# A graph layer's segment maximum: fewer nodes by chunk scans, more by slots, and an iota of 96 columns between gathers

## The chip, the core and the metric

One core of one Trainium2 chip runs the whole kernel. TensorE (PE in the profile, PEld for its weight loads), VectorE (DVE), ScalarE (ACT), GpSimd (POOL) and SyncE (SP) run side by side and wait for one another through semaphores. The metric is the device time of one execution in microseconds (us); before the change it is 1135.02 us, the median of three runs (1132.8 to 1135.32).

## The reference

```
x_src = x[src];  x_dst = x[dst]                       # 100000 edges, sorted by dst
theta_x = (x_dst - x_src) @ theta_w.T + theta_b
phi_x = x_src @ phi_w.T + phi_b
e = relu(theta_x + phi_x)                             # 100000 x 256
out = segment_max(e, dst, num_segments=6250)
out = where(isfinite(out), out, 0.0)
return layernorm(x + out)
```

`x` has 6250 rows (nodes) of 256 floats. Within one node's segment `x_dst` is the same, so the kernel doesn't compute an edge at a time. It computes `b = x @ (phi_w - theta_w).T + theta_b + phi_b` and `a = x @ theta_w.T` once for each node; a node's result is `max(0, a[node] + max of b[src] over its edges)`, and 0 where it has no edges. What remains is an irregular maximum: for each of 6250 nodes the elementwise maximum over the rows of `b` that its edges (16 on average) name.

## The kernel before

The line numbers are those of the kernel before. Two methods share the nodes out, and some leftovers of the second form a third stream of work.

*By chunk scans (part 1).* The first `N1` = 6250 - 128 x 32 = 2154 nodes. Their edges lie in `dst` order; each of the 128 partitions takes 275 edges in a row (`FIRST_STEPS`, `T1`). In step t every partition gathers the row of `b` that its edge t names (`gather`, L467, an indirect DMA issued by POOL, one descriptor a partition), and DVE takes the running maximum with the row of the step before (`run`, L722); a column of `caps_1` cuts the running maximum off where a new node begins. Eight steps form a group (`STEPS`, `gather_group` L490, `group_1` L728), which fills one of seven tiles of a ring (`RING`), and is written to `maxima_1` in DRAM by SP. Five of the 35 groups (`X_GROUPS`) don't wait for `b_rows`: they gather rows of `x` before it exists and are multiplied by the weights on chip (`b_of`, L663). A segment that crosses from one partition to the next is put right at the end (`chunk_heads`, `tails_1`, `heads_1` L829: one gather from `maxima_1`, one maximum, one scatter back).

*By slots.* The last 4096 nodes, 32 for each partition (`TILES`). A window of `dst` (640 entries a partition, `WINDOW`, gathered by `gather_run`, L475) tells each partition where its nodes begin: `begin` (L623 to L632) counts the entries below each of 33 limits by one ACT operation of sign and sum for each. Then one gather for each of the 32 node columns brings a table of up to 36 source numbers a node (`table_i`, `R` = 36). The rows of `b` are cut into 17 *slots* of 375 rows. For a slot, `choice` (L877) finds for every node the lowest source that lies in it, and `wanted` (L912) writes these choices to DRAM as a row of 4096 numbers. `slot_part` (L939) then fetches the chosen rows, for 1024 nodes at a time, by matmul instead of by DMA: SP broadcasts the 1024 numbers over the partitions (`want`), DVE (L949) and ACT (L951, L952) turn them into one-hot matrices (`hot`), PE multiplies the slot's 375 rows (`terms`, two parts of the float32 value for accuracy) with them (L959, 24 matmuls of 512 columns), and DVE takes the maximum into `acc` (L970), which holds the result transposed. A slot is loaded by `slot_terms` (L926) into `raw` and split by ACT and DVE. 17 slots of 4 pieces of 1024 nodes are 68 parts.

*The list.* Where a node has a second source in the same slot, `choice` leaves it over. `list_pieces` (L980) packs the leftovers of each partition into a list of up to 240 (`LIST`); `group_2` (L1044) gathers and scans these in 30 groups of 8, as in part 1.

*Rows.* `rows_of` (L1051) computes `a` for up to eight tiles of 128 nodes, gathers the nodes' maxima, joins in `acc` and adds `x`; `normalise` (L1096) does the layernorm and writes `out`. `node_place` (L762) and `places_1` find, for part 1's 17 tiles, where in `maxima_1` a node's maximum lies.

The order of issue on each engine is that of the program; a tile framework adds the waits. The preparation (up to about L700) makes the tables on DVE, ACT and POOL while PE makes `b_rows`. Then the schedule (L1120 to L1193) interleaves by hand: the nine `choice` calls with two part-1 groups each and one slot part in the first; `list_pieces` with a slot part for each of its pieces; the rest of the part-1 groups at 1.2 slot parts a group (`PACE`); the list groups at 1.2 slot parts a group, with the tail work of part 1 in between; what is left of the slot parts; and last the rows of the slot nodes (in shares of 8, 8, 8, 4, 2, 1 and 1 tiles).

```
1152    places_1()
1153    carried = tails_1()
1154    lists = list(range(0, LIST, STEPS))
1155    for i in range(2):
1156        group_2(lists.pop(0))
1157        fetch_parts(1)
1158    heads_1(carried)
```

Of the kernel before, what the change touches and what calls it, by code (L numbers as in the profile page):

```python
# [52 lines left out]
RING = 7  # L53
GENERAL_STEPS = 17
FIRST_STEPS = 275
X_GROUPS = 5
X_BEFORE = 2
TILES = 32
LIST = 240
WINDOW = 640  # L60
# [5 lines left out]
PACE = 1.2  # L66
# [339 lines left out]
def gnn_kernel(ctx: ExitStack, tc: tile.TileContext, x, src, dst, theta_w, theta_b, phi_w, phi_b, out):  # L406
# [4 lines left out]
    Q = N // P  # L411
    LEFT = N - P * Q
    NT = Q + 1
    XQ = 4
# [8 lines left out]
    NB = N // ROWS  # L423
    NS = -(-NB // KB)
# [4 lines left out]
    assert D == 2 * P and LEFT > 0 and LEFT1 > 0 and Q % XQ == 0 and OWN % CW == 0  # L429
    assert (P - 1) * T + 1 < E <= P * T and N < ID_MASK and P * T <= EDGES and E + 8 * P <= EDGES  # L430
    assert N == NB * ROWS and SLOT * NS < ABSENT and KB * P <= SLOT and WINDOW <= 8 * P and P * T1 < E
    assert LIST % STEPS == 0 and TILES <= 32
# [12 lines left out]

    x_main = x[: P * Q, :].rearrange("(p q) d -> p q d", q=Q)
    b_main = b_rows[: P * Q, :].rearrange("(p q) d -> p q d", q=Q)
    b_block = b_rows.rearrange("(b r) d -> r b d", r=ROWS)


    x_1 = x[: P * Q1, :].rearrange("(p q) d -> p q d", q=Q1)
    x_2 = x[N1:, :].rearrange("(p q) d -> p q d", q=TILES)
    out_1 = out[: P * Q1, :].rearrange("(p q) d -> p q d", q=Q1)
    out_2 = out[N1:, :].rearrange("(p q) d -> p q d", q=TILES)
    maxima_1t = maxima_1[: P * T1, :].rearrange("(p t) d -> p t d", t=T1)
    maxima_2t = maxima_2[: P * LIST, :].rearrange("(p t) d -> p t d", t=LIST)

    def iota(t, step, base, per_partition):
        nc.gpsimd.iota(
            t,  # L460
            pattern=[[step, t.shape[1]]],
            base=base,
            channel_multiplier=per_partition,
            allow_small_or_imprecise_dtypes=True,
        )

    def gather(to, table, offsets):  # L467
        nc.gpsimd.indirect_dma_start(  # L468
            out=to, out_offset=None, in_=table, in_offset=bass.IndirectOffsetOnAxis(ap=offsets, axis=0)
        )  # L470

    def gather_run(to, table, offsets):

        n = to.shape[1]
        nc.gpsimd.indirect_dma_start(  # L475
            out=to,
            out_offset=None,
            in_=flat(table, 0, [[n, EDGES // n], [1, n]]),
            in_offset=bass.IndirectOffsetOnAxis(ap=offsets, axis=1),
        )  # L480
# [16 lines left out]
    for i in of_x[:X_BEFORE]:  # L497
        gather_group(i, x)
# [28 lines left out]

    weights = const.tile([P, 2, KC, D], FP, name="weights")
    bias = const.tile([P, 1, D], FP, name="bias")

# [13 lines left out]
    with (  # L544
# [4 lines left out]
        with tc.If(n_unsorted > 0):  # L549
            sort_edges(nc, sort, ps_sort, src, dst, src_list, dst_list, ident)  # L550
            load_chunks(nc.sync, dst_i, dst_list, T, EDGES)
            load_chunks(nc.sync, dst_1, dst_list, T1, EDGES)
            load_rows(nc.scalar, src_1, src_list, P * T1)
            for i in of_x[:X_BEFORE]:
                gather_group(i, x)
# [51 lines left out]
    accs = body.enter_context(tc.tile_pool(name="accs", bufs=1))  # L607
    acc = accs.tile([P, KC, OWN], FP, name="acc")
    index = body.enter_context(tc.tile_pool(name="index", bufs=1))
    dst_w = index.tile([P, WINDOW], I32, name="dst_w")  # L610
    gather_run(dst_w, dst_list, edge0_i)
    for i in of_x[X_BEFORE:]:
        gather_group(i, x)
# [9 lines left out]
    BATCH = 8  # L623
    for j0 in range(0, TILES + 1, BATCH):
        j1 = min(j0 + BATCH, TILES + 1)
        for j in range(j0, j1):
            junk = index.tile([P, WINDOW], BF, name="junk")
            nc.scalar.activation(  # L628
                junk, local, AF.Sign, bias=halves[:, j : j + 1], scale=-1.0, accum_out=sums[:, j : j + 1]
            )  # L630
        nc.vector.tensor_scalar(begin[:, j0:j1], sums[:, j0:j1], 0.5, 0.5 * WINDOW, op0=ALU.mult, op1=ALU.add)
# [8 lines left out]

    with (
        tc.tile_pool(name="prep", bufs=1) as prep,
        tc.tile_pool(name="x_in", bufs=3) as x_in,
# [5 lines left out]
        for i, w in enumerate((theta_w, phi_w)):  # L649
            nc.sync.dma_start(w_in[:, i], w.rearrange("(c p) k -> p c k", p=P))  # L650
        biases = prep.tile([P, 2, D], FP, name="biases")
        for i, b in enumerate((theta_b, phi_b)):
            nc.sync.dma_start(biases[:, i, :], flat(b, 0, [[0, P], [1, D]]))
        nc.vector.tensor_add(bias[:, 0, :], biases[:, 0, :], biases[:, 1, :])
        nc.vector.tensor_sub(w_in[:, 1], w_in[:, 1], w_in[:, 0])
        for i in (1, 0):
            for c in range(KC):
# [3 lines left out]
                nc.vector.tensor_copy(weights[:, i, :, c * P : (c + 1) * P], ps[:, 0])  # L661

        def b_of(to, rows):  # L663

            n = rows.shape[1]
            ps = ps_t.tile([P, 2, KC, P], FP, name="ps_xt")
            for i in range(n):
                for k in range(KC):
                    nc.tensor.transpose(ps[:, i, k, :], rows[:, i, k * P : (k + 1) * P], ident)
            x_t = prep.tile([P, 2, KC, P], FP, name="x_t", bufs=3)  # L670
            nc.scalar.copy(x_t[:, :n], ps[:, :n])  # L671
            ps = ps_b.tile([P, 2, D], FP, name="ps_b")
            for i in range(n):
                for k in range(KC):
                    nc.tensor.matmul(  # L675
                        ps[:, i, :], x_t[:, i, k, :], weights[:, 1, k, :], start=(k == 0), stop=(k == KC - 1)
# [3 lines left out]
        for q in range(0, NT, XQ):  # L680
            n = min(XQ, NT - q)
            b_sb = b_out.tile([P, XQ, D], FP, name="b_sb")
            x_q = x_in.tile([P, XQ, D], FP, name="x_q")
            if q < Q:
                nc.sync.dma_start(x_q, x_main[:, q : q + XQ, :])
            else:
                nc.vector.memset(x_q[:, 0, :], 0.0)
                nc.sync.dma_start(x_q[:LEFT, 0, :], x[P * Q :, :])
# [3 lines left out]
            if q < Q:  # L692
                nc.scalar.dma_start(b_main[:, q : q + XQ, :], b_sb)
            else:
                nc.scalar.dma_start(b_rows[P * Q :, :], b_sb[:LEFT, 0, :])
        for i in of_x:
            for k in range(0, STEPS, 2):
                rows = ring_tiles[i][:, k : k + 2, :]
# [15 lines left out]
    ps_fetch = fetch.enter_context(tc.tile_pool(name="ps_fetch", bufs=3, space=PSUM))  # L714
    last = {1: None, 2: None}
# [113 lines left out]
    def heads_1(carried):  # L829
        heads = work.tile([P, D], FP, name="heads", bufs=1)  # L830
        at_heads = bass.IndirectOffsetOnAxis(ap=head_i[:, 0:1], axis=0)
        nc.gpsimd.indirect_dma_start(out=heads, out_offset=None, in_=maxima_1, in_offset=at_heads)
        nc.vector.tensor_tensor(heads, heads, carried, op=ALU.max)
        nc.gpsimd.indirect_dma_start(out=maxima_1, out_offset=at_heads, in_=heads, in_offset=None)
# [10 lines left out]
    BATCH_S = 2  # L845

# [6 lines left out]
    def sources():  # L853
        nc.vector.tensor_copy(source.rearrange(by_rank, r=R), table_i.rearrange("p j r -> p r j"))
        floor_of(work_1, source, ROWS)
        floor_of(work_2, work_1, KB)
        nc.vector.scalar_tensor_tensor(source, work_1, float(P - ROWS), source, op0=ALU.mult, op1=ALU.add)
        nc.vector.scalar_tensor_tensor(source, work_2, float(SLOT - KB * P), source, op0=ALU.mult, op1=ALU.add)
        nc.gpsimd.iota(
            rank.rearrange(by_rank, r=R),  # L860
            pattern=[[1, R], [0, TILES]],
            base=0,
            channel_multiplier=0,
            allow_small_or_imprecise_dtypes=True,
        )
# [6 lines left out]
        nc.vector.scalar_tensor_tensor(work_1, source, float(-ABSENT), work_2, op0=ALU.add, op1=ALU.mult)  # L872
        nc.vector.tensor_scalar(padded, work_1, float(ABSENT), None, op0=ALU.add)
        nc.vector.memset(unused, 1)


    def choice(s0):  # L877
# [17 lines left out]
        at = index.tile([P, BATCH_S, 1, TILES], I16, name="at")  # L895
        for i in range(n):
            blocks = min(KB, NB - (s0 + i) * KB)
            nc.vector.tensor_scalar(
                at[:, i, 0, :], low[:, i, :W], (blocks - 1) * P + ROWS, None, op0=ALU.min
            )  # L900
        nc.vector.tensor_copy(chosen[:, s0 : s0 + n, :], at[:, :n, 0, :])
# [24 lines left out]
    def slot_terms(s):  # L926

        blocks = min(KB, NB - s * KB)
        f = raw
        even = ROWS // 16 * 16  # L930
        nc.sync.dma_start(f[:even, :blocks, :], b_block[:even, s * KB : s * KB + blocks, :])
        nc.sync.dma_start(f[even:ROWS, :blocks, :], b_block[even:, s * KB : s * KB + blocks, :])
        terms = terms_of[s] = slots.tile([P, PARTS, KB, D], FR, name="terms")
        nc.scalar.copy(terms[:, 0, :blocks], f[:, :blocks])
        nc.vector.tensor_tensor(
            terms[:, 1, :blocks], f[:, :blocks], terms[:, 0, :blocks].bitcast(FP), op=ALU.subtract
        )

    def slot_part(s, c):  # L939
        if c == 0:  # L940
            slot_terms(s)
        blocks = min(KB, NB - s * KB)
# [4 lines left out]
        for b in range(blocks):  # L947
# [5 lines left out]
        for h in range(KC):  # L953
            ps = ps_fetch.tile([P, CW], FP, name="ps_f")
            n = blocks * PARTS
# [23 lines left out]

    def list_pieces():  # L980
        left_over = index.tile([P, BATCH_S, TR], I16, name="in_slot")[:, 0, :]
        nc.vector.scalar_tensor_tensor(left_over, padded, float(ABSENT), unused, op0=ALU.is_lt, op1=ALU.mult)
        valid, count, place, name = work_1, work_2, rank, source
# [7 lines left out]
        nc.gpsimd.iota(  # L991
            place, pattern=[[1, TR]], base=1, channel_multiplier=0, allow_small_or_imprecise_dtypes=True
        )
        nc.vector.tensor_tensor(count, place, count, op=ALU.subtract)
        nc.vector.tensor_tensor(count, count, valid, op=ALU.mult)
        distance = place.bitcast(I32)
        nc.vector.tensor_copy(distance, count)
        nc.vector.tensor_scalar(distance, distance, 19, None, op0=ALU.logical_shift_left)
        nc.gpsimd.iota(
            name.rearrange(by_node, r=R),  # L1000
            pattern=[[1 << ID_BITS, TILES], [0, R]],
            base=1,
            channel_multiplier=0,
            allow_small_or_imprecise_dtypes=True,
# [30 lines left out]
        has = work.tile([P, TILES], FP, name="has_2")  # L1035
# [190 lines left out]
```

## Time and profile before

| what | value | from |
|---|---|---|
| runs | 1132.8, 1135.02, 1135.32 us | three timed runs |
| profiled execution | 1127.47 us, span 1125.6 us | one execution, the one that all rows below are from |
| granted TensorE clock | 0.788 | mean over the span |
| slot matmuls, PE, L959 | 1600 of 436 ns, 444.9 us | groups |
| gathers of `b_rows` for part 1, POOL, L468 | 235 of 1184 ns, 278.3 us | groups |
| gathers of `b_rows` for the list, POOL, L468 | 240 of 986 ns, 236.6 us | groups |
| scans, DVE, L722 | 513 of 478 ns, 244.3 us | groups |
| maxima into `acc`, DVE, L970 | 128 of 1215 ns, 155.5 us | groups |
| one-hot matrices, ACT, L951 and L952 | 132 of 1145 and 132 of 1050 ns, 280.0 us | groups |
| one-hot matrices, DVE, L949 | 68 of 748 ns, 50.9 us | groups |
| counts, ACT, L628 | 33 of 830 ns, 27.4 us | groups |
| wait of POOL ahead of L832's gather | 23.4 us, for a write of `maxima` | groups |

The page draws the span in 40 slices of 28.1 us, a digit being the busy tenths of a slice (9 is 90% or more):

```
PE   0466893585147403295829328578185785986273
PEld 0355783364135302173607216456164664764262
DVE  1221693799978621184758118276165584994164
ACT  0256220564114210075655105276254463830175
POOL 6735377488888777554524754667555756204500
```

The stages lie so: preparation up to about 143 us, choice and list with the first groups of part 1 to about 396, the rest of part 1's groups to about 542, the list groups to about 1020, the rows of the slot nodes to the end. How to read the prediction's rows: a group's row gives an instruction's line, engine, operation and tile, how often it ran, its busy sum and mean; a row of waits gives what the engine's instruction waited for, "remote" and "issue" standing for time that the profile can't put down to another instruction's end; a row of a stretch gives its busy time on each engine and the count of instructions in it.

### The profile page before, as it was taken

The numbers are of one execution on the slowest core, as the hardware profiler recorded it, in microseconds if no ns is written. First come the engines' busy times: TensorE is split into PE (matmuls) and PEld (weight loads), VectorE is DVE, ScalarE is ACT, GpSimd is POOL, SyncE is SP. The second block draws the span as 40 slices with busy tenths as digits, with TensorE's granted clock in tenths as the row PEclk, the third lists the DMA queues.
The fourth block names the chain that finished last, engine by engine and source line by source line (L and its number), as shares of the span: only waits on it lengthen the run. The fifth ranks groups of instructions, "written<-read, shape, count | busy, mean of one in ns | idle before, by whom it ended". The sixth has DMA issues, their size and how long they took to land. (4 is left out here: it accounts for less than half of the span.)

```text
span 1125.6 us, 9291 instructions
## 1 busy us (share of the span) xinstructions
PE 651.4 (58%) x2557; PEld 503.6 (45%) x2557; DVE 630.7 (56%) x1309; ACT 429.2 (38%) x680; POOL 640.3 (57%) x622
## 2 busy tenths in 40 slices
PE   0466893585147403295829328578185785986273
PEld 0355783364135302173607216456164664764262
DVE  1221693799978621184758118276165584994164
ACT  0256220564114210075655105276254463830175
POOL 6735377488888777554524754667555756204500
PEclk9888996787668756596959757889586977988696
DMA  6445365477455645264738627566275665735222
GB/s 213 128 138 165 113 193 179 140 254 238 169 173 190 201 144 166 77 221 128 229 122 290 188 81 226 165 220 213 85 238 182 219 202 189 240 144 215 80 99 92
DMA packets 63082, 195.61 MB, mean 174 GB/s; under 512 B 14071, under 2 KB 22795, under 8 KB 53515
## 3 DMA queue, kind: packets, MB, share of 16 engines
q1 hardware_dynamic: 32207, 112.01, 28.3%
q0 software_dynamic: 28272, 75.14, 23.2%
q10 hardware_dynamic: 2540, 7.75, 1.8%
q8 instruction: 23, 0.38, 0.1%
q14 instruction: 40, 0.33, 0.1%
HBM read 114.27 MB, written 81.38 MB: 174 GB/s over the span
## 5 line engine op out<-in xcount | busy, mean ns | idle before, releaser
L959 PE MATMUL ps_f<-hot,terms 128*128 128x512 f32 x1600 | 444.9, 436 | 293.7 <-DVE hot L949 123.0
L959 PEld LDWEIGHTS ps_f<-hot,terms 128*128 128x128 f32 x1600 | 334.6, 213 | 392.5 <-issue 222.9
L468 POOL DMA_INDIRECT g<-b_rows,src x235 | 278.3, 1184 | 118.1 <-issue 67.7
L468 POOL DMA_INDIRECT g<-b_rows,list_src x240 | 236.6, 986 | 148.2 <-issue 72.3
L970 DVE TENSOR_TENSOR acc<-acc,ps_f 128x1024 f32<-128x1024 f32 x128 | 155.5, 1215 | 252.5 <-remote 228.7
L951 ACT ACTIVATE hot<-want,minus_row 128x1024 fp32r<-128x1024 f16 x132 | 146.1, 1145 | 323.3 <-remote 200.3
L722 DVE SCALAR_TENSOR_TENSOR g<-g,caps 128x256 f32<-128x256 f32 x513 | 244.3, 478 | 27.5 <-DMA g<-b_rows,src 9.7
L952 ACT ACTIVATE hot<-hot 128x1024 fp32r<-128x1024 f32 x132 | 133.9, 1050 | 0.4
L675 PE MATMUL ps_b<-weights,x_t 128*128 128x256 f32 x356 | 94.1, 421 | 55.0 <-ACT x_t L671 43.0
L468 POOL DMA_INDIRECT g<-maxima,place x49 | 47.1, 961 | 109.3 <-issue 62.0
L675 PEld LDWEIGHTS ps_b<-weights,x_t 128*128 128x128 f32 x356 | 72.9, 211 | 73.5 <-ACT x_t L671 48.2
L1077 PE MATMUL ps_e<-weights,x_t 128*128 128x256 f32 x128 | 37.4, 440 | 39.2 <-ACT x_t L1073 37.3
L671 ACT COPY x_t<-ps_xt 128x512 f32<-128x512 f32 (+1 forms) x45 | 24.9, 577 | 76.3 <-remote 31.1
L949 DVE TENSOR_SCALAR hot<-want,row_id 128x1024 fp32r<-128x1024 f16 x68 | 50.9, 748 | 1.3 <-ACT hot L952 1.3
L475 POOL DMA_INDIRECT table_i<-src_list,begin_i x32 | 30.2, 944 | 34.0 <-DVE begin_i L632 24.5
L468 POOL DMA_INDIRECT g<-in_x_dram,src x40 | 38.5, 964 | 15.9 <-issue 11.3
L1077 PEld LDWEIGHTS ps_e<-weights,x_t 128*128 128x128 f32 x128 | 25.9, 213 | 47.1 <-ACT x_t L1073 41.2
L678 DVE TENSOR_TENSOR b_sb<-ps_b,bias 128x512 f32<-128x512 f32 (+1 forms) x25 | 16.7, 677 | 52.3 <-PE ps_b L675 22.9
L1104 ACT ACTIVATE squares<-g,r 128x256 bf16<-128x256 f32 x49 | 24.3, 498 | 47.7 <-issue 39.8
L628 ACT ACTIVATE junk<-local,halves 128x640 bf16<-128x640 f32 x33 | 27.4, 830 | 32.1 <-DVE b_sb L678 16.3
L1087 DVE TENSOR_TENSOR g<-g,ps_e 128x512 f32<-128x512 f32 (+1 forms) x17 | 11.1, 655 | 48.7 <-PE ps_e L1086 23.7
L1073 ACT COPY x_t<-ps_e 128x512 f32<-128x512 f32 (+1 forms) x17 | 9.4, 553 | 61.0 <-PE ps_e L1071 38.3
(194 smaller groups left out, 511.1 us busy)
## 6 DMA issues: line engine op xcount, KB each, us to landing
maxima<-g SPq DMA_DIRECT2D x64, 1024.0 KB
want<-chosen_rows SPq DMA_DIRECT2D x68, 256.0 KB
x_q<-in_x_dram SPq DMA_DIRECT2D x12, 512.0 KB
b_rows<-b_sb ACTq DMA_DIRECT2D x12, 512.0 KB
raw<-b_rows SPq DMA_DIRECT2D x16, 336.0 KB
g<-in_x_dram SPq DMA_DIRECT2D x5, 1024.0 KB
out_dram<-g SPq DMA_DIRECT2D x5, 1024.0 KB
g<-b_rows,list_src POOLq DMA_INDIRECT x240
```

Of the source, the lines that this page charges most:

```text
L468: nc.gpsimd.indirect_dma_start(out=to, out_offset=None, in_=table, in_offset=bass.IndirectOffsetOnAxis(ap=offsets, axis=0))
L475: nc.gpsimd.indirect_dma_start(out=to, out_offset=None, in_=flat(table, 0, [[n, EDGES // n], [1, n]]), in_offset=bass.IndirectOffsetOnAxis ...
L628: nc.scalar.activation(junk, local, AF.Sign, bias=halves[:, j : j + 1], scale=-1.0, accum_out=sums[:, j : j + 1])
L671: nc.scalar.copy(x_t[:, :n], ps[:, :n])
L675: nc.tensor.matmul(ps[:, i, :], x_t[:, i, k, :], weights[:, 1, k, :], start=(k == 0), stop=(k == KC - 1))
L722: nc.vector.scalar_tensor_tensor(g[:, k, :], last[part], caps[:, t : t + 1], g[:, k, :], op0=ALU.min, op1=ALU.max)
L949: nc.vector.tensor_scalar(hot[:, b, :], want, row_id[:, b : b + 1], None, op0=ALU.is_equal)
L951: nc.scalar.activation(hot[:, b, :], want, AF.Abs, bias=minus_row[:, b : b + 1], scale=1.0)
L952: nc.scalar.activation(hot[:, b, :], hot[:, b, :].bitcast(FP), AF.Relu, bias=1.0, scale=-1.0)
L959: nc.tensor.matmul(ps[:, w : w + 512], terms[:, part, b, h * P : (h + 1) * P], hot[:, b, w : w + 512], start=(i == 0), stop=(i == n - 1),)
L970: nc.vector.tensor_tensor(to, to, ps, op=ALU.max)
L1077: nc.tensor.matmul(a[:, i, :], x_t[:, 2 * i + c, :], weights[:, 0, c, :], start=(c == 0), stop=(c == KC - 1))
```

## The change

Nodes are shared out otherwise: 40 a partition go by slots (5120 instead of 4096), and 1130 instead of 2154 by chunk scans, of 146 steps instead of 275. With that the window grows from 640 to 800 entries, the list from 240 to 288, a slot has five pieces of 1024 nodes instead of four (85 parts instead of 68), and part 1 has 9 tiles of nodes instead of 17. Three groups of part 1 gather `x` (five before), one of them ahead of the branch that sorts unsorted edges (two before).

POOL's order is written out: `in_turn` ties each gather, and each iota behind it, to the one before by a dependency without a semaphore, and behind every gather stands an iota of 96 columns into a tile that nothing reads:

```diff
+    pause = const.tile([P, PAUSE], FP, name="pause")
+    latest = [None]
+
+    def in_turn(one):
+        if latest[0] is not None:
+            after = mybir.DependencyInfo(mybir.DependencyClass.NoSync, mybir.DependencyReason.DATA)
+            tc.add_manual_dep(one.ins, latest[0], after, reason="GpSimd's order")
+        latest[0] = one.ins.name
+
+    def indirect(out, in_, in_offset=None, out_offset=None):
+        in_turn(nc.gpsimd.indirect_dma_start(out=out, out_offset=out_offset, in_=in_, in_offset=in_offset))
+
     def gather(to, table, offsets):
-        nc.gpsimd.indirect_dma_start(
-            out=to, out_offset=None, in_=table, in_offset=bass.IndirectOffsetOnAxis(ap=offsets, axis=0)
-        )
+        indirect(to, table, bass.IndirectOffsetOnAxis(ap=offsets, axis=0))
+        in_turn(iota(pause, 1, 0, 0))
```

`gather_run` gets the same two lines, and the two iotas of `list_pieces` take their turn in this order. The constants:

```diff
-RING = 7
-FIRST_STEPS = 275
-X_GROUPS = 5
-X_BEFORE = 2
-TILES = 32
-LIST = 240
-WINDOW = 640
+RING = 4
+RING_2 = 7
+FIRST_STEPS = 146
+X_GROUPS = 3
+TILES = 40
+LIST = 288
+WINDOW = 800
...
-PACE = 1.2
+PACE = 2.2
+PAUSE = 96
```

Part 1 has a ring of four tiles; the list and the rows have one of seven (`ring_2`), in the room that the index tables leave when the list is made. Half of the counting moves to DVE, in batches of ten limits instead of eight:

```diff
+    BATCH, BY_SIGNS = 10, 5
...
+            junk = index.tile([P, WINDOW], BF, name="junk" if j < jm else "junk_v")
+            if j < jm:
+                nc.scalar.activation(
+                    junk, local, AF.Sign, bias=halves[:, j : j + 1], scale=-1.0, accum_out=sums[:, j : j + 1]
+                )
+            else:
+                nc.vector.tensor_scalar(
+                    junk, local, halves[:, j : j + 1], None, op0=ALU.is_le, op1=ALU.add, accum_out=begin[:, j : j + 1]
+                )
```

A slot's rows lie otherwise in the partitions: three contiguous rows of `b` in each, instead of three blocks of 125 rows, so that each partition's piece of the load is one run (`slot_terms`); `sources` computes a source's place in its slot accordingly, with one operation more, and its iota of ranks moves ahead into the preparation. Each slot part now has three blocks, the last slot's too.

`b_rows` is made in shares of up to four node tiles of part 1 and of the slot nodes each (`shares`, `node_rows`), instead of 48 tiles over all the nodes and one rest; the columns of `weights` for `b` and `a` change places. The last rows go in five shares of eight tiles.

The schedule:

```diff
     for s0 in range(0, NS, BATCH_S):
         choice(s0)
         wanted(s0)
-        for _ in range(2):
-            group_1(groups_1.pop(0))
-        if s0 == 0:
-            fetch_parts(1)
+        next_group_1(1)
     chunk_heads()
...
     for i, _ in enumerate(list_pieces()):
         if i % 2:
-            group_1(groups_1.pop(0))
-        fetch_parts(1)
-    pace = 0.0
-    while groups_1:
...
+            next_group_1(1)
+    tables.close()
+    ring_2 = body.enter_context(tc.tile_pool(name="ring_2", bufs=RING_2, side="right"))
+    while groups_1 or todo:
+        next_group_1(2)
     places_1()
     carried = tails_1()
...
+    heads = heads_1(carried)
+    for i in range(LIST // STEPS):
+        group_2(i * STEPS)
         pace += PACE
-        while pace >= 1.0:
-            fetch_parts(1)
-            pace -= 1.0
-        if len(lists) % 3 == 0 and (shares or waiting):
+        fetch_parts(int(pace))
+        pace -= int(pace)
+        if i in (3, 5):
+            next(heads, None)
+        if i > 6 and i % 3 == 0 and (early_shares or waiting):
```

`next_group_1(n)` issues a group of part 1, one `node_place` and n slot parts. `heads_1` is a generator now: its gather and its maximum come behind the fourth list group, its scatter behind the sixth (both behind the second before).

## The prediction

> **What bounds the kernel now.** I read the page's busy times first, then the engine-by-stretch table, then the waits, then PE's own timeline. No engine is the bound over the whole span:
>
> ```profile
> PE 651.4 (58%) x2557; PEld 503.6 (45%) x2557; DVE 630.7 (56%) x1309; ACT 429.2 (38%) x680; POOL 640.3 (57%) x622
> ...
> 0.00:143.00 143.00, 76.49 (x349) 62.45 (x350) 43.49 (x98) 44.46 (x95) 75.97 (x97) 0.92 0.48 149
> 143.00:396.00 253.00, 141.45 (x549) 109.62 (x547) 206.89 (x422) 83.20 (x99) 194.21 (x151) 0.77 0.59 194
> 396.00:542.00 146.00, 69.07 (x238) 51.25 (x239) 57.29 (x112) 47.18 (x77) 84.04 (x84) 0.68 0.49 152
> 542.00:1020.00 478.00, 312.91 (x1186) 239.30 (x1185) 280.40 (x519) 212.49 (x293) 255.19 (x259) 0.80 0.58 189
> 1020.00:1125.60 105.60, 51.48 (x242) 40.94 (x240) 42.65 (x161) 41.91 (x119) 30.89 (x32) 0.76 0.35 121
> ```
>
> The columns are length, busy PE, PEld, DVE, ACT, POOL, clock, DMA share, GB/s. Only 143 to 396 has a full engine (DVE, 82%). From 396 to 1020 everything is half idle, so the question is who waits for what:
>
> ```profile
> DVE acc L970 <- remote: 228.7, 21, 24.4
> PEld ps_f L959 <- issue: 222.9, 57, 32.3
> ACT hot L951 <- remote: 200.3, 12, 56.9
> ```
>
> The three columns are microseconds, times, longest. Two stretches (columns as above) and PE's timeline:
>
> ```profile
> 398.00:415.00 17.00, 0.00 (x0) 0.00 (x0) 0.00 (x0) 0.00 (x0) 12.78 (x14) 0.50 0.41 125
> 873.00:890.00 17.00, 17.00 (x77) 14.08 (x76) 13.69 (x23) 10.58 (x12) 13.13 (x13) 1.00 0.86 274
> ...
> 457.31 0.58 PE L959 MATMUL ps_f<-hot,terms 128*128 128x512 f32 x1 [1.50 <-issue]
> 460.11 0.59 PE L959 MATMUL ps_f<-hot,terms 128*128 128x512 f32 x1 [2.21 <-issue]
> 462.21 0.58 PE L959 MATMUL ps_f<-hot,terms 128*128 128x512 f32 x1 [1.51 <-issue]
> ```
>
> DVE and ACT wait over 200 us for something that the profile can't place, and PE's weight loads 223 us for nothing visible. The last lines show it: a matmul every 2.1 to 2.8 us with no wait for any engine. In that stretch POOL issues gathers back to back: 0.95 us each, 0.30 us between, period 1.25. DVE and ACT wait for PE's sums, and wake together at 476.92, 7.7 us after POOL's last gather (468.30 + 0.95). The same comes in the preparation (POOL's run ends at 58.5, PE's sums arrive at 62.4), at 197.3 and 201.3, at 519.4 and 522.9, and in the tail (1060.9, and 1069.5 for the next DVE sum). So uninterrupted gathers hold PE up. They need not: the 873 to 890 line has 13 gathers beside a full PE, at a mean period of 1.31, and from 142.97 to 165.42 sixteen gathers of period 1.40, stretched by DVE's work, run beside a PE busy 24.6 of 26 us; PE stalls when the period falls to 1.25. Which is cause and which effect the trace doesn't say: a stalled PE idles DVE, and then nothing stretches the gathers.
>
> **The change, part by part.**
>
> The pause. Every gather is followed by an iota of 96 columns (L464, held in order by in_turn). POOL's timeline prices it:
>
> ```profile
> 21.25 0.94 POOL L468 DMA_INDIRECT g<-in_x_dram,src  x1 [0.30 <-issue]
> 22.49 0.94 POOL L468 DMA_INDIRECT g<-in_x_dram,src  x1 [0.30 <-issue]
> ...
> 23.99 0.63 POOL L459 IOTA columns<- 128x128 f32 x3
> 24.57 0.23 POOL L459 IOTA ids<- 128x1 f32 x2
> ```
>
> Three iotas of 128 columns take 0.58 us from start to the next start, 0.193 each; small ones follow every 0.10; 96 columns interpolate to 0.165. A POOL operation starts as the gather before it ends (23.44, 58.52). Whether the 0.30 us ahead of the next gather stays is not shown: the period is 0.945 + 0.165 = 1.11 if it hides, 1.41 if it stays. I take 1.41, the nearer to what POOL shows after every gather. That is the period at which PE ran well. The new kernel gathers rows 483 times (146 + 288 + 49), this one 564 (40 + 235 + 240 + 49), so POOL needs 681 us instead of 705 at 1.25: nothing net. At 1.11 it would be 536, and no slower than now, but then the period is the one at which PE stalls.
>
> A rule speaks against it. The Trainium skill, SBUF — State Buffer, section "Who interferes with whom", says that VectorE's two-port modes and GpSimd exclude one another for a whole instruction. The rows agree in kind: gathers average 1.184 us beside the busy DVE of 143 to 542 and 0.986 later, against 0.945 alone. By the rule, were every second iota to sit out one 0.75 us compare (L949), the 299 gathers of the list stage would cost 112 us more, and the sum below would be 1103.
>
> Preparation (A), 143 us now up to the first gather of b_rows. POOL has 8 gathers ahead of the branch instead of 16: 8 x 1.41 = 11.3 against 19.9, with the rank iota of 1440 columns moved there (1.6), so 7 us earlier. The window gather (L475, now L484) stood behind 17 gathers (27.29 to 48.62); now it stands behind 8, at 20.3 + 11.3 = 31.6, and lands 3.5 later, at 35.1, not 52.1. Eight more x gathers end at 44.3, then 40 table gathers x 1.41 = 56.4, to 101. The counts that feed them no longer hold them up: of 10, five on ACT at 1.23 (0.83 x 800/640 + 0.19) and five on DVE, about 8 us against 14 of gathers. b_rows itself: 25 pairs of tiles at 2.31 us (5.45 + 1.47 for three pairs, 84.74 on) = 58 us from about 30, so 88 without stalls, 131 with today's (138 - 7). A = 104, bounds 101 and 131.
>
> Choice, list and first gathers (B), bound by DVE. Tables grow from 1152 to 1440 columns, 1.25 times: sources 16.8 (11.3 now, one more operation), choice 64 (54), list pieces 60 (48). Scans: 145 x 0.478 = 69. Corrections of x groups: 12 x 0.681 = 8. Of 85 slot parts (17 slots x 5), 22 are issued here (16 groups with one, 3 with two): 22 x 0.748 + 17 x 2 x 1.215 + 5 x 0.94 = 62. Node places and the rest 8. Sum 288; from 200 to 375, the stretch of the same work, DVE was busy 159.8 of 175 us, 91%, so 316. Bounds 288 and 346 (the stall of 170 to 200 stays, +30). The fixed order puts list_pieces' two iotas behind 48 gathers of b_rows, at most 48 x 1.65 = 79 us into B; DVE comes to them after choice, later, and waits for neither. POOL's 122 gathers at even 1.65 are 201, hidden; if DVE were free, PE's 22 x 6 = 132 would be next.
>
> List stage (C): 63 parts and 36 groups of gathers. What a part costs is read from two rows:
>
> ```profile
> 825.00:1000.00 175.00, 133.96 (x525) 105.27 (x524) 0.85 0.64 207
> ...
> 975.00:1000.00 25.00, 22.95 (x100) 18.65 (x99) 0.98 0.63 237
> ```
>
> These are the slot matmuls (L959), 24 a part. The second row gives 25 x 24/100 = 6.0 us a part with POOL nearly idle, the first 8.0 with stalls in it; 542 to 1020 gives 478 x 24/1044 = 11.0. Per group of 2.2 parts, PE needs 13.2 at 6.0; POOL 8 x 1.41 = 11.3; DVE 8 x 0.478 + 2.2 x (0.748 + 2 x 1.215 + 0.19) = 11.2; ACT 2.2 x 4.55 = 10.0. Four engines so nearly level don't overlap fully: I take 7.2, so 63 x 7.2 = 454; bounds 378 and 504 without stalls. POOL's 299 x 1.41 = 422 lies beside it. The parts run out after 29 of 36 groups, with POOL up to six groups ahead: 12 us of scans and the last write. The wait of 23.4 us (L832, POOL for the writes of maxima) goes, since that gather now stands behind four groups; DVE waits less for gathers in turn. The larger share of slots is 17 parts more than now (17 x 7.2 = 122), against 81 gathers and scans fewer.
>
> Tail (D): 105.6 now; without its stall (24.7 of DVE's idle time between 1042.6 and 1069.5) 81; four more pairs of tiles at 3.6 (1069.5 to 1104.3 for ten) 14; the last share has eight tiles, not one, to normalise (+8). D = 103, or 128 if the stall stays. The moved weights, contiguous rows of raw and the node places between groups cost nothing while PE and SP have slack (SP issues one transfer in 0.3 us); without that cover 9 places x 1.2 = 11 us of ACT come in.
>
> Sum: 104 + 316 + 454 + 12 + 103 = 989, and 1.9 outside the span (1127.47 - 1125.6): 991. The median of runs (1135.02) stands 0.7% over the profiled one, so 998.
>
> **Rivals.** (1) The stalls go, but the coupled engines hold 8.0 us a part: +50, and A 11 worse: 1052, 1059 as a run. For it: all four engines level, and gathers stretched by DVE. Against: 100 matmuls in 25 us happen (525 to 550 has 104 as well). (2) Slower: the pause doesn't release PE. Then A 131, B 346, D 128, and C between 36 x 15.9 = 574 (478 us for 30 groups now) and 63 x 11.0 = 693, mean 633: 131 + 346 + 633 + 12 + 128 + 2 = 1252, at least 1193. It decides from 9.4 us a part with the other stages mended (590 us in C), 8.1 with none. For it: no iota stands between two gathers anywhere in the trace, and 0.165 us is short beside stalls of 20 us. Against: PE at full work beside gathers of period 1.40. (3) That no pause is there: the changed kernel's POOL order has one behind each gather, so this has no chance.
>
> **How the numbers follow.** Forecast (930 to 1035) 0.55; rival 1 (1035 to 1125) 0.22; no change, within 0.2% (what this measurement can tell), 0.02; rival 2 0.21. Faster 0.77, same 0.02, slower 0.21. With C at its bound of 378 the sum is 104 + 316 + 378 + 12 + 103 + 2 = 915; four level engines won't reach that, and the lower end is 920. To leave out no more than 2 in 10 the upper end goes to 1150.
>
> **What would show it.** Right: gathers 1.4 us apart; "remote" waits of DVE's acc under 60 us; no lone matmuls 2 us apart; first b_rows gather near 104; list gathers from about 415; last slot matmul near 870; 6.5 to 8 us a part. Wrong: PE idle beside running gathers as at 398 to 415, or a part at over 9.4 us.

## The result, and the profile after

The changed kernel takes 1032.95 us (median of 1016.0, 1028.3, 1037.6 and 1039.0) beside 1133.91 for the kernel before. The ratio is 0.9016, with a 95% interval of 0.8919 to 0.9113; it is taken over the two quicker runs, since disturbed ones are left out, and so lies below 1032.95 / 1133.91 = 0.911. The profiled execution took 1037.60 us, with a span of 1035.2, near the upper end of the four. The forecast was 998, range 920 to 1150.

That is the result on this chip. The same two programs, run later on another one, came out the other way round (the ninth run below): 960.27 against 907.34, 5.7% *slower*. The experiments show what the change removes on the one and pays on the other; why the chips differ they don't show.

The page of the changed kernel, busy times and the groups that answer to those of before (line, engine, operation, count, busy us, mean ns, idle time before):

```profile
PE 715.9 (69%) x2901; PEld 565.0 (55%) x2901; DVE 691.0 (67%) x1262; ACT 486.1 (47%) x682; POOL 731.3 (71%) x1074
...
L988 PE MATMUL ps_f<-hot,terms 128*128 128x512 f32 x2040 | 542.8, 428 | 185.8 <-DVE hot L978 73.8
...
L484 POOL DMA_INDIRECT g<-b_rows,list_src x288 | 292.3, 1015 | 56.7 <-issue 47.0
L999 DVE TENSOR_TENSOR acc<-acc,ps_f 128x1024 f32<-128x1024 f32 x160 | 194.5, 1216 | 180.0 <-remote 121.5
...
L484 POOL DMA_INDIRECT g<-b_rows,src x122 | 186.3, 1527 | 51.8 <-issue 49.0
...
L464 POOL IOTA pause<- 128x96 f32 x525 | 131.8, 251 | 3.8
```

All engines do more in less time, though there are 81 scans fewer: the slot matmuls grew from 1600 to 2040 (PE 651.4 to 715.9 us), and 525 iotas of 0.25 us are new. What shrank is idle time. The waits of the changed kernel (engine, line, what for: us, times, longest; "remote" is time that the profile can't put down to another instruction's end):

```profile
ACT hot L980 <- remote: 127.6, 15, 20.7
DVE acc L999 <- remote: 121.5, 28, 13.5
...
POOL g L484 <- DMA maxima<-g: 56.1, 3, 40.8
```

Before, the first two were 200.3 (ACT) and 228.7 (DVE): 429 us of waiting for sums of PE that the profile can't place (*late sums* from here on) became 249. They are fewer, not gone. The third row is new, and costs PE nothing: GpSimd waits 40.8 us for a write of maxima after the last list gather, while PE is full (below).

By stage (length, busy PE, PEld, DVE, ACT, POOL, clock, DMA share, GB/s). The cuts are the first gather of `b_rows`, the first list gather, 860 us, and the last slot matmul:

```profile
0.00:140.70 140.70, 80.21 (x357) 65.88 (x358) 73.23 (x149) 37.60 (x72) 81.98 (x151) 0.88 0.45 138
140.70:383.50 242.80, 142.43 (x522) 108.77 (x520) 203.52 (x377) 99.85 (x149) 220.42 (x246) 0.79 0.52 164
383.50:860.00 476.50, 359.00 (x1375) 280.94 (x1376) 310.09 (x505) 243.99 (x265) 379.80 (x597) 0.85 0.65 205
860.00:938.00 78.00, 75.19 (x330) 60.92 (x328) 53.39 (x67) 51.97 (x52) 29.82 (x48) 1.00 0.54 176
938.00:1035.20 97.20, 59.10 (x323) 48.52 (x322) 50.82 (x167) 52.72 (x145) 19.25 (x32) 0.90 0.24 88
```

Against the prediction's terms: A 140.7 (104 forecast), B 242.8 (316), C with its last scans 476.5 + 78.0 = 554.5 (454 + 12), D 97.2 (103). In the list stage PE alternates between two conditions. The slot matmuls alone, in three stretches (length, busy PE, PEld, clock, DMA share, GB/s):

```profile
525.00:550.00 25.00, 10.07 (x24) 7.35 (x24) 0.64 0.47 144
575.00:600.00 25.00, 25.00 (x112) 20.71 (x111) 1.00 0.82 266
850.00:875.00 25.00, 24.15 (x100) 19.82 (x101) 0.93 0.54 192
```

One part in 25 us, then 4.7 parts in 25 us, both beside running gathers; after 850 GpSimd has issued its last list gather and PE is full. How it passes from the one to the other is seen at 600. PE's timeline, GpSimd's and DVE's (start, duration, instruction, idle time before it and what ended it):

```profile
559.75 47.31 PE L988 MATMUL ps_f<-hot,terms 128*128 128x512 f32 x208
606.90 0.38 PE L1101 MATMUL ps<-ident,g 128*128 128x128 f32 x2
607.03 1.64 PE L988 MATMUL ps_f<-hot,terms 128*128 128x512 f32 x6
618.50 2.07 PE L1107 MATMUL ps<-weights,x_t 128*128 128x256 f32 x4 [9.83 <-ACT hot L980]
```

```profile
610.32 0.95 POOL L484 DMA_INDIRECT g<-b_rows,list_src  x1 [0.16 <-issue]
611.28 0.24 POOL L464 IOTA pause<- 128x96 f32 x1
611.67 0.96 POOL L484 DMA_INDIRECT g<-b_rows,list_src  x1 [0.16 <-issue]
```

```profile
610.92 1.22 DVE L999 TENSOR_TENSOR acc<-acc,ps_f 128x1024 f32<-128x1024 f32 x1 [3.11 <-remote]
612.06 1.52 DVE L744 SCALAR_TENSOR_TENSOR g<-g,caps 128x256 f32<-128x256 f32 x3
616.65 1.22 DVE L999 TENSOR_TENSOR acc<-acc,ps_f 128x1024 f32<-128x1024 f32 x1 [3.07 <-remote]
```

The last sum of PE's run ends at 559.75 + 47.31 = 607.06. DVE, idle for the last 3.07 us, takes it at 616.65, 9.6 us later. The trace also records the semaphore updates by which PE reports a sum. Up to about 593 the report lands 0.40 us after the sum's last matmul starts, which is the matmul's own time; the last three of this run land 2.0, 6.6 and 9.6 us after the end of theirs. So PE's reports fall behind while the gathers run on at 611.67 - 610.32 = 1.35 us; ACT and DVE then hand nothing over to PE, and PE stops. (The profile models the ends of matmuls, so it can't tell whether the sum or only its report was late.) It is the stall of before at a period of 1.25, later and shorter.

### The profile page after: what moved, and what is told of

It is laid out like the page before. It is cut to its first block, busy times and chain, and to the rows that moved or that the text cites. A ratio compares the mean times of both kernels' runs of the same rounds, so it can differ in the third digit from the quotient of the medians.

```text
span 1035.2 us, 10299 instructions
## 1 busy us (share of the span) xinstructions
PE 715.9 (69%) x2901; PEld 565.0 (55%) x2901; DVE 691.0 (67%) x1262; ACT 486.1 (47%) x682; POOL 731.3 (71%) x1074
## 4 chain that ended last, share of the span: by engine, by line
PE 34%; DVE 22%; another core or an unknown queue 13%; issue 13%; POOL 8%; ACT 5%; DMA 3%; ACTq 0%; DVEq 0%; POOLq 0%
PE ps_f L988 29%; POOL g L484 5%; DVE g L744 4%; PE ps_e L1107 2%; ACT hot L980 2%; DVE hot L978 2%; DVE junk_v L644 2%; DVE acc L999 2%; POOL pause L464 1%; DVE in_slot L927 1%; DVE lowest L915 1%; DVE b_sb L704 1%; DMA g<-b_rows,src 1%; ACT hot L981 1%
## 5 line engine op out<-in xcount | busy, mean ns | idle before, releaser
L988 PE MATMUL ps_f<-hot,terms 128*128 128x512 f32 x2040 | 542.8, 428 | 185.8 <-DVE hot L978 73.8
L988 PEld LDWEIGHTS ps_f<-hot,terms 128*128 128x128 f32 x2040 | 421.4, 210 | 301.3 <-issue 134.1
L980 ACT ACTIVATE hot<-want,minus_row 128x1024 fp32r<-128x1024 f16 x170 | 187.1, 1145 | 315.6 <-PE ps_f L988 149.9
L484 POOL DMA_INDIRECT g<-b_rows,list_src x288 | 292.3, 1015 | 56.7 <-issue 47.0
L999 DVE TENSOR_TENSOR acc<-acc,ps_f 128x1024 f32<-128x1024 f32 x160 | 194.5, 1216 | 180.0 <-remote 121.5
L744 DVE SCALAR_TENSOR_TENSOR g<-g,caps 128x256 f32<-128x256 f32 x432 | 207.0, 482 | 44.6 <-DMA g<-b_rows,list_src 25.2
L484 POOL DMA_INDIRECT g<-b_rows,src x122 | 186.3, 1527 | 51.8 <-issue 49.0
L981 ACT ACTIVATE hot<-hot 128x1024 fp32r<-128x1024 f32 x170 | 170.3, 1045 | 0.1
L464 POOL IOTA pause<- 128x96 f32 x525 | 131.8, 251 | 3.8
L1139 ACT ACTIVATE g<-g,r 128x256 f32<-128x256 f32 x49 | 25.3, 590 | 14.1 <-DVE r L1137 9.0
```

Source lines behind the costliest of these rows:

```text
L464: return nc.gpsimd.iota(t, pattern=[[step, t.shape[1]]], base=base, channel_multiplier=per_partition, allow_small_or_imprecise_dtypes=True,)
L484: in_turn(nc.gpsimd.indirect_dma_start(out=out, out_offset=out_offset, in_=in_, in_offset=in_offset))
L744: nc.vector.scalar_tensor_tensor(g[:, k, :], last[part], caps[:, t : t + 1], g[:, k, :], op0=ALU.min, op1=ALU.max)
L980: nc.scalar.activation(hot[:, b, :], want, AF.Abs, bias=minus_row[:, b : b + 1], scale=1.0)
L981: nc.scalar.activation(hot[:, b, :], hot[:, b, :].bitcast(FP), AF.Relu, bias=1.0, scale=-1.0)
L988: nc.tensor.matmul(ps[:, w : w + 512], terms[:, part, b, h * P : (h + 1) * P], hot[:, b, w : w + 512], start=(i == 0), stop=(i == n - 1),)
```

## The experiments

Each group of runs shared one chip and its own runs of the kernel before. Times are medians, and a 95% interval stands behind each ratio.

| run | change against the changed kernel | kernel before, us | this, us | ratio |
|---|---|---|---|---|
| 1 | no iota | 1141.06 | 1125.35 | 0.982 [0.972, 0.991] |
| 2 | 192 columns | 1141.06 | 985.95 | 0.863 [0.855, 0.871] |
| 3 | 288 columns | 1141.06 | 1020.05 | 0.892 [0.884, 0.899] |
| 4 | 384 columns | 1141.06 | 1046.70 | 0.916 [0.909, 0.922] |
| 5 | 1440 columns after every eighth | 910.69 | 969.92 | 1.063 [1.056, 1.070] |
| 6 | 160 columns | 910.69 | 979.45 | 1.075 [1.068, 1.082] |
| 7 | kernel before with 96 columns | 910.69 | 996.20 | 1.092 [1.085, 1.098] |
| 8 | 192 columns, rows first | 910.69 | 975.26 | 1.073 [1.065, 1.080] |
| 9 | none (the changed kernel) | 907.34 | 960.27 | 1.057 [1.055, 1.060] |
| 10 | as 5 | 907.34 | 969.99 | 1.071 [1.065, 1.077] |
| 11 | as 1 | 1137.42 | 1108.62 | 0.988 [0.972, 1.005] |
| 12 | as 5 | 908.57 | 971.17 | 1.071 [1.065, 1.077] |

Runs 1 to 4 and 11 were on chip 13, 5 to 8 on chip 14, 9 and 10 on chip 4, 12 on chip 5. The chip of the first comparison has no number on record.

**No iota (run 1).** The lines taken out, in `gather`, `gather_run` and `heads_1`:

```diff
-        in_turn(iota(pause, 1, 0, 0))
```

> The changed kernel without the iota behind each gather (the fixed order stays). Theory: PE's reports of finished sums reach DVE and ACT late whenever gathers follow one another in under about 1.43 us; in the changed kernel's trace the sums' users start 0.04 to 2 us after a sum's last matmul where eight gathers had a mean period of 1.45 us or more, and 5 to 29 us after it where the period was 1.35 to 1.42. Without the iota the period falls to 1.25, so nearly every stretch with gathers stalls: 11.0 us a slot part as in the kernel before, 68 parts in the list stage = 750 us, or at least 36 groups of 15.9 us = 572; the whole 1080 to 1280 us. Rival (the gain of the change comes from the other shares and from the fixed order, and the iota is only GpSimd time): 483 iotas are worth nothing or cost, so 1033 us or less, down to 1033 - 299 x 0.11 = 1000.

1125.35 us, ratio 0.982. Its waits:

```profile
ACT hot L977 <- remote: 206.9, 14, 31.8
DVE acc L996 <- remote: 196.4, 21, 28.1
```

403 us of waits for late sums, like the kernel before (429). Shares, order and schedule without the iota are worth 2% at most here: run 11 repeats this with a ratio of 0.988 and an interval that takes in 1. With the iota they were worth about 10% on the first chip. The theory's range has the time, and the rival's 1033 or less falls on this chip.

**Longer iotas (runs 2 to 4).** One constant:

```diff
-PAUSE = 96
+PAUSE = 192
```

> The changed kernel with an iota of 192 columns. From the trace an iota of 96 columns makes the period 1.36 us and one of 288 takes 0.39 instead of 0.23 us, so 192 columns make it about 1.44 to 1.46 without any stretching by DVE. Theory: this lies just over the limit, the stalls go nearly everywhere: 5.4 to 6 us a part, list stage about 305 gathers x 1.46 = 445 to 480 us instead of 554, the whole 930 to 970 us. Rival (the iota is only GpSimd time, or the stalls come of something else): 1033 us plus up to 483 x 0.09 = 43.

> The changed kernel with an iota of 288 columns, period about 1.52 us. Theory: no stalls beside gathers, but GpSimd's 305 gathers of the list stage take 464 us at least; the whole 940 to 980 us, and within 25 us of the one with 192 columns, on either side. Rival (only GpSimd time): 1033 to 1033 + 483 x 0.16 = 1110.

> The changed kernel with an iota of 384 columns, period about 1.62 us. Theory: still no stalls, GpSimd becomes the bound of the list stage (305 x 1.62 = 494 us) and of the stage before it; the whole 970 to 1010 us, slower than with 288 columns. Rival (only GpSimd time): 1033 to 1033 + 483 x 0.26 = 1160.

192 columns give a median period of 1.44 us (0.96 the gather, 0.31 the iota, 0.16 the gap) and 985.95 us, 47 us less than the changed kernel on the first chip. From the waits of run 2:

```profile
PE ps_f L988 <- DVE hot L978: 124.7, 37, 15.8
DVE g L744 <- DMA g<-b_rows,list_src: 115.7, 61, 26.2
...
ACT x_t L691 <- remote: 11.7, 4, 7.5
...
DVE b_sb L704 <- remote: 6.6, 3, 2.2
```

No row has `acc` or `hot` waiting for "remote" any more; now DVE waits for gathers. The last two rows are the only ones for "remote" that are left, 18 us in the preparation; with 288 and 384 columns there is none at all. So `acc` and `hot` wait 403, 249 and 0 us for late sums with 0, 96 and 192 columns. The direction is the theory's, the sizes are not: 986 instead of 930 to 970, then 1020 instead of 940 to 980 and 1047 instead of 970 to 1010. 986 lies below the rival's range, 1020 too; 1047 lies in it. I had priced a longer iota by the 305 gathers of the list stage. From 192 to 288 columns the period grows by 0.081 us and the time by 34 us, from 288 to 384 by 0.077 and 27: that is 420 and 350 gathers' worth, about the 410 gathers of `b_rows`, so GpSimd's queue is the bound nearly from the first of them to the last once the stalls are gone. From there on a longer iota is only GpSimd's time, as the rival has it; for the first 192 columns it is wrong.

**One iota for eight gathers (run 5), 160 columns (run 6), the iota alone (run 7).** Run 5 counts the gathers:

```diff
+    def pause_every_8():
+        gathers[0] += 1
+        if gathers[0] % 8 == 0:
+            in_turn(iota(pause, 1, 0, 0))
```

Run 7 puts `pause`, `in_turn` and the iota of 96 columns into the kernel before and changes nothing else.

> The changed kernel with one iota of 1440 columns (about 1.5 us) after every eighth gather in place of one behind each. GpSimd is kept from gathers for as long as with 192 columns behind each (8 x 0.19 us longer than without any), but the eight gathers between two iotas have a period of 1.25 us. Theory (the spacing of single gathers decides): the stalls come back, 1060 to 1130 us. Rival (the share of time in which GpSimd issues gathers decides, or the iota lets PE catch up): as with 192 columns behind each, 970 to 1000 us.

> The changed kernel with an iota of 160 columns; by the measured medians of 1.36 us (96 columns) and 1.44 (192) its period is about 1.41. Theory with a sharp limit near 1.43: stalls come and go as with 96 columns, since a gather stretched by DVE lifts the period over the limit and only a stall lets it fall back: 990 to 1035 us. Rival (a gradual effect, every ns between gathers helps or costs alike): between 986 and 1033 in proportion, 1002.

> The kernel before with the iota of 96 columns behind each gather and GpSimd's order tied as in the change; the shares of nodes, the lists and the schedule of before. With the shares of after the iota was worth 1125 - 1033 = 92 us. Theory: here it is worth as much or somewhat less, as fewer parts (68) can stall and there are 564 gathers: 1030 to 1090 us. Rival (the iota helps only together with the new shares, for 564 gathers at 1.36 us are 767 us of GpSimd): 1110 to 1160.

969.92, 979.45 and 996.20 us. Run 5 seems to go to the rival, run 6 to neither, run 7 beyond the theory; but the kernel before took 910.69 us beside them, not 1135. On this chip none of the three has a single wait for "remote". In run 5's gathers of 1.25 us (GpSimd's timeline, and the slot matmuls around it):

```profile
440.28 0.95 POOL L484 DMA_INDIRECT g<-b_rows,list_src  x1 [0.30 <-issue]
441.53 0.94 POOL L484 DMA_INDIRECT g<-b_rows,list_src  x1 [0.30 <-issue]
442.78 0.95 POOL L484 DMA_INDIRECT g<-b_rows,list_src  x1 [0.30 <-issue]
443.73 1.36 POOL L464 IOTA pause<- 128x1440 f32 x1
```

```profile
440.00:465.00 25.00, 24.68 (x109) 20.17 (x108) 1.00 0.82 274
```

PE is full beside them. So these runs tell nothing of the spacing that brings the stall. Run 7 does show something: where nothing stalls, the iota and the fixed order only cost, 996.20 - 910.69 = 85 us. The period of its gathers is 1.36 us instead of 1.25, which by 564 gathers makes 60 us; what the rest is, is not shown.

**Rows first (run 8).** The first operation on the table of sources is tied, on DVE, behind the last addition that makes `b_rows`:

```diff
+        last_row = added[0].ins.name
...
+        tc.add_manual_dep(turned.ins, last_row, behind_rows, reason="rows first")
```

> 192 columns behind each gather, and the first operation on the table of sources tied behind the last addition that makes b_rows, on DVE. Theory: the preparation lasted 138 us instead of the 104 of the prediction because DVE, in order, waits some 11 us for the last piece of the table with the additions for b_rows queued behind it, which stops PE; tied, the first gather of b_rows comes 8 to 14 us earlier, and as GpSimd is the bound from there on, the whole gains 5 to 12 us: 974 to 981. Rival (DVE's tables bound the stage, not b_rows): the first gather earlier, the whole within 5 us of 986 or slower.

975.26 us. The first gather of `b_rows` comes at 113.3 us, against 137.6 in run 6 on the same chip and 138.2 in run 2. That is more than the 8 to 14 expected, and it shows what held the preparation up. Of these 24 us the whole shows only the 4 between runs 6 and 8, which differ by 32 columns too: the next stages are longer, B 253.1 against 241.9, C 512.9 against 505.2. What part of the gain the longer iota hides wasn't tried, so the whole time decides nothing between theory and rival.

**The changed kernel and run 5 again (runs 9 and 10), run 1 again (11), run 5 a third time (12).** No new edits.

> The changed kernel as it is, beside the kernel before on one chip. In the last runs the kernel before took 911 us on another chip than the 1135 of the first, and no kernel there showed waits for late sums of PE, at a period of 1.25 us either. Theory (the stalls beside closely spaced gathers are a matter of the chip; the change's gain is the removal of these stalls): where the kernel before takes about 911, the changed one has no stalls to remove and pays for 483 iotas and 17 more slot parts: 955 to 985 us, slower than before; where it takes about 1135, again 1016 to 1040. Rival (something else differed in those runs): faster than the kernel before, ratio 0.88 to 0.95, wherever it runs.

> One iota of 1440 columns after every eighth gather, as once before (970 us on the chip where the kernel before took 911, without late sums at 1.25 us within each eight). Theory (spacing decides where the chip has the stalls): where the kernel before takes about 1135, stalls come back, 1060 to 1130 us; where it takes about 911, 970 again. Rival (a break now and then is enough): 970 to 1000 on both.

> The changed kernel without the iota, which took 1125 us beside a kernel before of 1141 (ratio 0.98). Where the kernel before takes about 908: theory (there is no stall beside gathers of 1.25 us there, the iota is only GpSimd's time): faster than with the iota (960) by the part of 305 x 0.11 = 34 us that lies on the path, 915 to 945 us, with no wait of DVE for late sums over 5 us; what remains over 908 is the price of the other shares. Rival (the iota is worth something there too): 960 or more. Where the kernel before takes about 1135 it is 1125 again.

> One iota of 1440 columns after every eighth gather, a third time; on the chips where the kernel before took 911 and 907 it took 970 both times. Where the kernel before takes about 1137: theory (it is the spacing of single gathers that holds PE's reports up) the eight gathers of period 1.25 between two iotas stall PE again, 1060 to 1130 us, with DVE's waits for late sums over 100 us; rival (a break of 1.5 us now and then lets PE catch up) 970 to 1010 us and no such waits.

Run 9 decides between its theory and its rival: 960.27 beside 907.34, slower by 5.7%, as the theory had it. Its waits:

```profile
DVE g L744 <- DMA g<-b_rows,list_src: 110.6, 59, 24.6
...
DVE acc L999 <- PE ps_f L988: 29.4, 25, 2.2
```

The same program with the same period of 1.36 us waits 249 us for late sums on the first chip, and no row of any engine is for "remote" here. Run 11 fell on chip 13 again: 1108.62, with 178.5 (ACT) and 173.7 (DVE) of late sums, so that chip stalls on both visits. Runs 10 and 12 fell on chips where the kernel before takes 907 to 909, and repeat run 5 without deciding anything: theory and rival agree there. Whether one break for eight gathers would free PE on a chip that stalls stays open, and so do run 7 and the shares without the iota on the respective other kind of chip.

## Why the prediction was right, and where not

**The bound.** That closely issued gathers hold PE's sums back, and that this rather than any engine bounded the kernel, was read from the trace of before and is shown on chip 13: with no iota `acc` and `hot` wait 403 us for late sums and the kernel takes 1125 us, with 192 columns they wait none and it takes 986. The two programs differ in the iota alone, so how GpSimd issues its gathers is the cause and not, as the prediction left open, an effect of a stalled PE. Whether the distance of each gather to the next counts, or GpSimd's free time as a whole, stays open, as runs 5, 10 and 12 fell on chips that don't stall. What the trace could not tell is that this goes with the chip. On three others, visited once each, the kernel before takes 907 to 911 us. The 226 us between are about DVE's 228.7 us of "remote" waits; a trace of the kernel before on such a chip, which would show it directly, wasn't taken. A lower clock of chip 13 is not the reason: the granted clock there is 0.825 with no iota and 0.879 with 192 columns, beside 0.883 in run 9, so it drops with the stalls.

**The pause.** I took a period of 1.41 us, between bounds of 1.11 and 1.41; it is 1.36, as the gap shrinks from 0.30 to 0.16 behind an iota while the iota takes 0.24 and not 0.165. The step that failed is "that is the period at which PE ran well": 1.36 is not. The prediction's own sign of being wrong, PE idle beside running gathers, is there at 525 to 550, and the waits of `acc` that should have been under 60 us are 121.5. PE runs well for some 50 us while DVE's work stretches the gathers, then a stretch of 1.36 begins a stall, which mostly lasts until GpSimd has to wait for something. At 1.44 the waits of `acc` and `hot` are gone, and 18 us are left in the preparation. The expectations' limit of about 1.43 was read from how long after its last matmul each sum is used. It does not come out of that trace: some sums are used within 0.1 us at a mean period of 1.35 to 1.42, and some over 14 us late at 1.45 or more. The measure also counts DVE's own queue (in run 9, without a late sum, sums are used over 5 us late too), so I give no limit beyond these periods.

**The rule on shared ports.** The Trainium skill, SBUF — State Buffer, section "Who interferes with whom", says that DVE in its two-port modes and GpSimd block one another for a whole instruction. With every second iota sitting out a comparison of DVE I had put 112 us on that in the list stage. The runs show no such price: the mean iota took 0.251 us, the median one 0.231, some 0.02 x 299 = 6 us. The gathers beside a busy DVE do lengthen, to 1.527 us in B.

**A, 104 forecast, 140.7 measured.** Outside its bounds. The sum "58 us from about 30, so 88 without stalls" took the pairs of tiles as free to follow one another. DVE, in order, met the first operation on the table with additions for `b_rows` queued behind it (DVE's timeline, then PE's):

```profile
111.19 1.44 DVE L888 CAST source<-table_i 128x1440 f32<-128x1440 int32 x1 [7.83 <-DMA table_i<-src_list,begin_i]
112.55 0.68 DVE L704 TENSOR_TENSOR b_sb<-ps_b,bias 128x512 f32<-128x512 f32 x1
```

```profile
113.37 0.98 PE L701 MATMUL ps_b<-weights,x_t 128*128 128x256 f32 x3 [3.37 <-DVE b_sb L704]
```

and run 8 without this reaches 113.3. The stalls are not it: run 9, which has none, reaches 134.5. The order of the instructions in DVE's queue, rather than their sum, would have told.

**B, 316 forecast, 242.8 measured.** The single terms were good: choice 63.4 us of DVE (64 forecast), list pieces 57.7 (60), sources 15.1 (16.8). But the sources fall into A, 5.5 of the 22 slot parts slip into C, and the stage ends for GpSimd before DVE is through. GpSimd, which I had hidden at 122 x 1.65 = 201, was the bound, busy 220.4 us besides the gaps behind its iotas: 122 gathers in 242.8 us are 1.99 each.

**C, 466 forecast, 554.5 measured.** 68.5 parts in place of 63 (1644 matmuls / 24), at 554.5 / 68.5 = 8.1 us instead of 7.2. Run 9, with no stalls, has 494.1 / 68.5 = 7.2. So 7.2 is what the coupled engines give, as chosen; 28 us of the error are there without stalls, from the 5.5 parts more, and the 60 between 494.1 and 554.5 are stalls that I had taken as gone. "The parts run out after 29 of 36 groups" is wrong: after the last list gather, at 849, PE works for 89 us on parts. DVE had done 75.5 of the 85 parts at its last list scan, 1.6 a group, in run 9 exactly so too. The order in which an engine gets its work is thus not that in which the program issues it, as I had said of the kernel before and gone by here; what sets it is not shown.

**D, 103 forecast, 97.2 measured.** Right. The errors of A, B, C and D are +37, -73, +88 and -6, and their sum is only 46 us by luck: B's error hid most of C's. Rival 1's number (1059, from 8.0 us a part) fits C's 8.1, but its reason, coupled engines, doesn't: run 9 shows that they need 7.2. Rival 2, slower because the pause doesn't free PE, gave the wrong cause for what came on chip 4: there the change is slower since nothing was to be freed. Its ground that no iota stands between two gathers anywhere in the trace isn't so: those that priced the pause stand between the gathers at 22.49 and 27.29.

## What to carry to other kernels

A wait that ends at nothing the profile can name is a thing to measure on a second chip before one pays for its removal. Filler between instructions is worth its price only where it removes a stall; here 47 us were still to be had by 96 more columns where the chip stalls, and on another chip the filler and the fixed order cost the kernel before 85 us. When several engines are almost level, forecast the order of instructions in each queue, not only the sums.

## What the runs showed of the hardware

On chip 13 beside gathers that GpSimd issues 1.25 us apart, and on the first beside 1.25 and 1.36, PE's reports of finished sums come microseconds late; on chips 4, 5 and 14 they don't. They catch up mostly where GpSimd has to wait, and the same program takes 1141 or 911 us. Why chips differ in this isn't settled by these runs. Neither the period of the gathers (1.25 and 1.36 on both kinds) nor their median length (0.946 and 0.949 us at 1.25, 0.959 and 0.957 at 1.36) tells the two kinds apart.

Where the chip stalls the versions rank 192 columns (986), 288 (1020), 96 (1033 on the first), 384 (1047), none (1125 and 1109), before (1137 and 1141); on the others before (907 to 911), 96 columns (960), one iota for eight gathers (970), 160 columns (979), before with 96 columns (996). No version that was run on both kinds is best on both.
